# Two graph-attention layers on one Trainium2 core: holding the turning of each group's score row behind a partial sum on VectorE

## Chip, cores and metric

The kernel runs on one core of a Trainium2 chip. The metric is the device time of one launch in microseconds, taken as the median of several runs. All arithmetic is float32.

## What is computed

The input `x` is 64 graphs of 256 nodes with 512 features; `adj` is one 256 x 256 adjacency matrix for all of them. Two layers follow, each of the form `x = x + layer(relu(layernorm(x)), adj)`. Cut to what matters:

```python
# layer 0: additive attention
h = X @ W                                     # 512 -> 256
e = h @ a[0] + swap(h @ a[1])                 # one score per node pair
e = leaky_relu(e, 0.2) + NEG * (1 - adj)
alpha = softmax(e)
out0 = concat(alpha @ h, h)
# layer 1: multi-head attention, 8 heads of 64
q, k, v = X @ Wq.T + bq, X @ Wk.T + bk, X @ Wv.T + bv
attn = softmax(where(adj == 0, -inf, q @ k.T / 8))
out1 = (attn @ v) @ Wo.T + bo
```

## The kernel before

**Tiling.** The 64 graphs go through in 32 groups of two (`GB = 2`), numbered g = 0 to 31. The work of three groups is interleaved: while step (g, b) does layer 1's attention of graph b of group g, it also does the q, k, v projections of group g+1, layer 0 of group g+2 and the first norm of group g+3. The order inside a step is written out by hand: the strings `steps` (near the end of `bounded`) hold one letter for each piece of work, and the loop over them calls the next piece of the generator that the letter names ("s" is a piece of `first_layer(g + 2)`, "f" one of `fold`, "u" one of `project`, "o" one of `outputs`, "n" one of `first_norm`, "m" one of `mask_pairs`). Each group therefore has two half-steps, b = 0 and b = 1. A scheduler then decides the final order on each engine. Where the code calls `after(instruction, name)` or `not_sooner(...)`, an instruction is fixed behind another one on its engine without a semaphore.

**The row sums of the softmax (`fold`).** The masked exponentials `p` are summed over partitions in a detour. For each quad of four heads SyncE writes them to device memory (`rows<-p`), reads them back in another layout (`parts<-rows`, four transfers), GpSimd adds the parts in two additions (`add`), and VectorE turns the result and reduces it (`sum_up`: `parts<-parts`, a transpose of 128x256, then `compact<-parts`). The list `fold_last` then names that reduction. There are two quads, so two sums: only after `sum_up(0, ...)` does `fetch(1)` issue the second quad's four transfers. In the half b = 0 both quads' parts lie in the buffer with the tag `e`, of which there is one. The same buffer holds layer 0's score matrix (`both`, in the profile `e`).

**The score row of layer 0 (`first_products`, `score_rows`, `first_layer`).** For g >= 2, layer 0's product H = X W is made in seven block products; two VectorE additions write its last blocks (`H<-ph,kept_h`). Then `score_rows(g)` turns columns 0 to 7 of H on VectorE (`rows<-H`, a transpose of 128x32), SyncE writes the row to device memory (`line<-rows`), waits until it has landed, and reads it back to all partitions (`own<-line`). ScalarE then makes four pieces of `e` from it (`e<-own,H`), VectorE takes the leaky maximum (`e<-e`), ScalarE the exponential, and VectorE applies the mask (`e<-e,maskT`).

**Order around it.** On SyncE every transfer here is fixed in the program's order: `parts<-rows` of the second quad, then `line<-rows`, `own<-line`, `passed<-xt` (the first norm of group g+3), and `out_dram<-x`. In the program, `sum_up(0, ...)` of step g stands before `score_rows(g + 2)`; the scheduler places `rows<-H` and the statistics of the next norm (`st<-x`, `mv<-st`, `factor<-mv`) ahead of it on VectorE, except for group 2 (and, for group 3, ahead of its reduction only). On ScalarE the exponentials of the attention scores (`p<-sc`) are fixed behind `edge_last`, the exponential of `e`. The scores `sc` are made by TensorE in PSUM banks: five turn under the tag `turn`, and one of the eight score banks of a half-step is the separate `held2`.

`score_rows` is called in `first_products`, right after the addition that writes the last block of H:

```python
        product(second, 4, False)
        vector.tensor_add(part(1, 0), second, p16)
        owns[g] = score_rows(g)
        residual_from(1)
```

Of the kernel before, what the change touches and what calls it, by code (L numbers as in the profile page):

```python
# [57 lines left out]
def bounded(  # L58
# [56 lines left out]
    def after(instruction, name):  # L115

        tc.add_manual_dep(
            instruction.ins, name,
            mybir.DependencyInfo(mybir.DependencyClass.NoSync, mybir.DependencyReason.DATA),
            reason="the engine's order",  # L120
        )

    def not_sooner(engine, operation, *args, **kwargs):

        last = engine.last
        after(getattr(engine, operation)(*args, **kwargs), last)
# [143 lines left out]
    put_last, norm_last, edge_last, sums_last, turn_last, fold_last = [], [], [], [], [], []  # L270
# [350 lines left out]
    def score_rows(g):  # L621
        rows = small.tile([P, GT, 8], F32, tag="rows", name=f"rows_{g}", bufs=2)
        last = vector.last
        turned = vector.transpose(rows.rearrange("p t c -> p (t c)"), H[:, :, 0:8])
        for other in [last, *fold_last] if g == 2 else [last]:
            after(turned, other)
        line = dram.tile([P // 8, S], F32, tag="line", name=f"line_{g}")
        not_sooner(sync, "dma_start", line, rows.rearrange("p t c -> p (t c)")[::8, :])
        own = att.tile([P, P // S, GT, S], F32, tag="r", name=f"own_{g}", bufs=1)
        not_sooner(  # L630
            sync, "dma_start", own.rearrange("p k t j -> p (k t j)"),
            line.rearrange("(o k) j -> o (k j)", o=1).to_broadcast([P, TOK]),
        )
        return own.rearrange("p k t j -> p t k j")

    def first_products(g):
# [53 lines left out]
# [4 lines that stand above are left out]
        yield  # L694
# [908 lines left out]
```

## Time and profile before

| | |
|---|---|
| Median of 3 runs | 2425.27 us (2424.95 to 2428.83) |
| Profiled execution: its own time | 2427.43 us |
| Its span in the trace | 2425.8 us |
| TensorE busy | 2391.4 us (99%) |
| VectorE busy | 1712.9 us (71%) |
| GpSimd busy | 1431.3 us (59%) |
| ScalarE busy | 1020.1 us (42%) |
| `rows<-H` (VectorE transpose 128x32) | 30 times, 210 ns mean |
| `parts<-parts` (VectorE transpose 128x256) | 124 times, 439 ns mean |
| `compact<-parts` (VectorE reduction) | 124 times, 420 ns mean |
| `line<-rows`, `own<-line` (SyncE transfers) | 30 times each |

The page gives, for each engine, the time it was busy; then the chain of work that ended last, followed back from the last instruction; then the costliest groups of instructions, with the idle time of the engine before them and what ended it. A timeline line gives the start, the duration, the engine, the operation, what it writes and reads, and in brackets the idle time of the engine just before it. PE is TensorE, DVE is VectorE, ACT is ScalarE, POOL is GpSimd, SPq is the queue of SyncE.

### The profile page before, as it was taken

What the parts mean: (1) busy time and instruction counts of PE and PEld (TensorE: products, weight loads), DVE (VectorE), ACT (ScalarE), POOL (GpSimd) and SP (SyncE); (2) the same over time, 40 slices, a digit from 0 to 9 for tenths busy, and PEclk for the clock granted to TensorE, in tenths of its full rate; (3) what the DMA queues carried; (4) which work ended last, traced back from release to release, by engine and by line L of the source; (5) the groups of instructions that cost most, each with busy time, mean ns of one, the idle gap of its engine ahead of it and who ended that gap; (6) DMA issues with size and microseconds to landing.
All of it is one profiled execution on the core that took longest, in us unless ns stands there. A gap on an engine that the chain in (4) does not pass through costs nothing.

```text
span 2425.8 us, 43056 instructions
## 1 busy us (share of the span) xinstructions
PE 2391.4 (99%) x15828; PEld 2005.6 (83%) x15828; DVE 1712.9 (71%) x3345; ACT 1020.1 (42%) x2017; POOL 1431.3 (59%) x1290
## 2 busy tenths in 40 slices
PE   9999999999999999999999999999999999999998
PEld 8888888888888888888888888888888888888886
DVE  7577776676766777667767677776677676777665
ACT  5444444343443443444444434444344344343431
POOL 4565555755656655566555565565665566655652
PEclk9999999999999999999999999999999999999999
DMA  5344445454445544455444545444554445454331
GB/s 187 126 139 144 144 133 154 145 159 140 132 139 149 169 143 134 130 161 148 144 144 134 154 144 160 147 130 134 152 166 144 135 135 158 143 156 138 112 114 45
DMA packets 271864, 343.49 MB, mean 142 GB/s; under 512 B 25376, under 2 KB 217120, under 8 KB 271648
## 3 DMA queue, kind: packets, MB, share of 16 engines
q1 hardware_dynamic: 271648, 340.69, 46.0%
q8 instruction: 126, 2.06, 0.4%
q14 instruction: 90, 0.74, 0.1%
HBM read 176.95 MB, written 163.64 MB: 140 GB/s over the span
## 4 chain that ended last, share of the span: by engine, by line
PE 87%; DMA 4%; DVE 3%; ACT 3%; issue 2%; POOL 1%; SPq 0%; ACTq 0%; DVEq 0%; POOLq 0%
PE pq L137 16%; PE pv L137 16%; PE py L137 14%; PE pk L137 14%; PE sc L137 8%; PE ph L137 8%; PE pr L137 6%; PE po L137 4%; ACT e L35 2%; DMA passed<-xt 1%; DMA own<-line 1%; DVE e L35 1%; DVE p L35 1%; ACT p L35 1%; DMA line<-rows 0%
## 5 line engine op out<-in xcount | busy, mean ns | idle before, releaser
L35 POOL TENSOR_TENSOR p<-p 128x512 f32<-128x512 f32 x248 | 392.9, 1598 | 453.6 <-DVE p L35 451.0
L35 ACT ACTIVATE xn<-x,factor 128x512 f32<-128x512 f32 x256 | 194.7, 807 | 384.4 <-POOL factor L35 377.3
L35 DVE TENSOR_TENSOR p<-p,maskT 128x1024 f32<-128x1024 f32 x254 | 347.5, 1389 | 3.2 <-ACT p L35 3.2
L35 POOL TENSOR_TENSOR parts<-parts 128x512 f32<-128x512 f32 x248 | 248.0, 1000 | 158.8 <-DMA parts<-rows 147.4
L35 DVE TENSOR_TENSOR x<-py,x 128x256 f32<-128x256 f32 x448 | 184.4, 412 | 179.8 <-PE py L137 173.6
L35 ACT ACTIVATE p<-sc 128x512 f32<-128x512 f32 x512 | 256.9, 620 | 88.5 <-PE sc L137 72.1
L137 PE MATMUL sc<-q,k 64*128 64x256 f32 x2048 | 255.1, 386 | 22.0 <-ACT p L35 22.0
L137 PEld LDWEIGHTS sc<-q,k 64*128 64x128 f32 x2048 | 201.3, 186 | 76.4 <-ACT p L35 34.2
L137 PE MATMUL py<-wo_sb,oT 128*128 128x256 f32 x1024 | 262.4, 379 | 0.6 <-DVE oT L35 0.6
L137 PE MATMUL pk<-hT,wk_sb 128*128 128x256 f32 x1024 | 244.8, 382 | 0.0
L137 PE MATMUL pq<-hT,wq_sb 128*128 128x256 f32 x1024 | 240.1, 382 | 1.1 <-ACT hT L35 0.7
L137 PE MATMUL pv<-wv_sb,hT 128*128 128x256 f32 x1024 | 236.8, 379 | 0.0
L137 PE MATMUL pr<-p,v 128*32 128x256 f32 x4096 | 234.2, 380 | 0.0
L137 PEld LDWEIGHTS pq<-hT,wq_sb 128*128 128x128 f32 x1024 | 191.8, 190 | 36.7 <-issue 10.3
L137 PEld LDWEIGHTS py<-wo_sb,oT 128*128 128x128 f32 x1024 | 194.2, 190 | 28.2 <-DVE oT L35 1.1
L137 PEld LDWEIGHTS pk<-hT,wk_sb 128*128 128x128 f32 x1024 | 189.7, 190 | 33.3 <-issue 9.9
L137 PEld LDWEIGHTS pv<-wv_sb,hT 128*128 128x128 f32 x1024 | 194.6, 190 | 26.5
L137 PEld LDWEIGHTS pr<-p,v 128*32 128x32 f32 x4096 | 126.7, 110 | 97.8 <-issue 18.2
L35 POOL TENSOR_TENSOR factor<-factor,rexp 128x2 f32<-128x2 f32 (+1 forms) x132 | 117.9, 893 | 150.2 <-DVE factor L35 149.8
L137 PE MATMUL py<-wo_sb,o_sums 128*128 128x256 f32 x768 | 197.6, 380 | 0.5 <-DVE x L35 0.5
L137 PE MATMUL pv<-wv_sb,sums 128*128 128x256 f32 x768 | 184.3, 383 | 2.2 <-ACT kept_v L35 2.2
L137 PE MATMUL pq<-sums,wq_sb 128*128 128x256 f32 x768 | 181.5, 379 | 0.0
(150 smaller groups left out, 4075.8 us busy)
## 6 DMA issues: line engine op xcount, KB each, us to landing
passed<-xt SPq DMA_DIRECT2D x124, 512.0 KB, 3.8
moved<-passed SPq DMA_DIRECT2D x496, 128.0 KB, 3.4
rows<-p SPq DMA_DIRECT2D x124, 512.0 KB, 3.4
parts<-rows SPq DMA_DIRECT2D x496, 128.0 KB, 3.0
x<-in_x_dram SPq DMA_DIRECT2D x64, 512.0 KB, 4.4
out_dram<-x SPq DMA_DIRECT2D x62, 512.0 KB, 4.4
own<-line SPq DMA_DIRECT2D x30, 256.0 KB, 3.5
wq_sb<-in_L_gnn_Wq_dram SPq DMA_DIRECT2D x2, 512.0 KB, 9.1
```

Source lines behind the costliest of these rows:

```text
L35: instruction = getattr(self.engine, operation)(*args, **kwargs)
L137: in_order(nc.tensor.matmul(*args, **kwargs))
```

## The change

`score_rows` already holds the turning of the row behind the last reduction of `fold` (`fold_last`) for group 2. The change does this for every group from 2 on.

```diff
         turned = vector.transpose(rows.rearrange("p t c -> p (t c)"), H[:, :, 0:8])
-        for other in [last, *fold_last] if g == 2 else [last]:
+        for other in [last, *fold_last] if g >= 2 else [last]:
             after(turned, other)
```

When `score_rows` is called, `fold_last` names the reduction of the first quad of the half b = 0. No instruction is added or removed. In the built program the order on TensorE, ScalarE, GpSimd and SyncE is the same as before; on VectorE it differs in 29 places, one for each of the groups 3 to 31. For groups 4 to 30 it goes from

```
rows<-H, st<-x, mv<-st, st<-x, mv<-st, factor<-mv x2, parts<-parts, compact<-parts, x<-py, k<-pk
```

to

```
parts<-parts, compact<-parts, rows<-H, st<-x, x<-py, mv<-st, st<-x, mv<-st, factor<-mv x2, k<-pk
```

For group 3 only `compact<-parts` moves, from behind the first `st<-x` to just ahead of `rows<-H`. For group 31, which has no norm beside it, `rows<-H` moves from just ahead of `parts<-parts` to just behind `compact<-parts`.

## The prediction

> **What bounds the kernel now.** I began with the page. TensorE is busy for 99% of the span, and the group of score products is the one large group on it with idle time of its own.
>
> ```profile
> PE 2391.4 (99%) x15828; PEld 2005.6 (83%) x15828; DVE 1712.9 (71%) x3345; ACT 1020.1 (42%) x2017; POOL 1431.3 (59%) x1290
> ...
> L137 PE MATMUL sc<-q,k 64*128 64x256 f32 x2048 | 255.1, 386 | 22.0 <-ACT p L35 22.0
> ```
>
> The reader sees that only what makes TensorE wait can move the time, and that a wait of the scores for ScalarE's exponentials is such a thing. Next I read the chain of waits in order of time over one group (step g = 15, where the score row of group 17 is made).
>
> ```profile
> 1201.61 3.65 PE sc L137 x32
> 1205.26 7.10 PE pq L137 x32
> ...
> 1234.37 3.40 DMA passed<-xt
> ...
> 1237.86 1.72 ACT e L35 x4
> ...
> 1240.87 0.59 ACT p L35
> ...
> 1241.50 2.26 PE sc L137 x15
> ```
>
> In the half b = 0 the 32 score products run through in 3.65 us. In the half b = 1 the chain leaves TensorE, goes over a transfer, `e` and the first exponential, and comes back to the 17th score product. In TensorE's timeline the scores of b = 1 start at 1238.57 and the matmul behind them at 1243.69: 5.12 us, so 1.47 us are lost. (The page's 22.0 us counts less, since the ends of matmuls are modelled; I use distances between starts.) I read this distance in every half-step. In b = 0 it is always 3.65 from group 2 on; in b = 1 it is 4.59 to 5.81 for g = 2 to 28, so 0.94 to 2.16 lost, mean 1.34, in all 36.2 us; for g = 0 and 1 the loss is 0.71 and 0.70, and for g = 29 it is 0.09.
>
> Then VectorE and SyncE's queue before that wait.
>
> ```profile
> 1225.99 0.21 DVE L35 STREAM_TRANSPOSE rows<-H 128x32 f32<-128x32 f32 x1
> 1226.13 0.65 DVE L35 BATCH_NORM_STATS2 st<-x 128x6 f32<-128x512 f32 x1
> ...
> 1227.83 0.62 DVE L35 TENSOR_SCALAR factor<-mv 128x2 f32<-128x2 f32 x2
> 1228.36 0.43 DVE L35 STREAM_TRANSPOSE parts<-parts 128x256 f32<-128x256 f32 x1
> 1228.82 0.42 DVE L35 TENSOR_REDUCE compact<-parts 128x8 f32<-128x256 f32 x1
> 1229.16 0.42 DVE L35 TENSOR_TENSOR x<-py,x 128x256 f32<-128x256 f32 x1
> ```
>
> ```profile
> 1229.32 1.73 SPq L35 DMA_DIRECT2D parts<-rows  x4
> 1231.09 0.53 SPq L35 DMA_DIRECT2D line<-rows  x1
> 1233.98 0.34 SPq L35 DMA_DIRECT2D own<-line  x1
> 1234.37 0.43 SPq L35 DMA_DIRECT2D passed<-xt  x1
> ```
>
> The row is turned at 1226.2, but its transfer stands in SyncE's queue behind the second quad's four fetches, and those wait for the first quad's reduction, which ends at 1229.24. So turning the row early gains nothing: 0.08 us after the reduction the queue moves, and `line` is issued 4.9 us after the row was ready. `e` starts at 1237.86. The chain names `passed<-xt`, but `e` does not read it; `own` takes 3.0 to 3.9 us to land (its tile's view), so its landing, 1237.0 to 1237.9, is what I take as the end of that wait.
>
> **What the skill says.** The Trainium skill, "Perfetto Trace Analysis", § Optimization Strategy, says to look for gaps on the limiting engine and trace who releases them, and that a gap that keeps repeating can mean a lack of SBUF or PSUM. Agreed: here it repeats in 27 groups and the 17th score product waits for a score bank to be read. "DMA: Bandwidth & Descriptors", § Anatomy of one DMA, says that a wait on a semaphore is done by the issuing sequencer ahead of dispatch. Agreed: `own` leaves 2.89 us after `line` and `passed` right behind it, so one waiting transfer holds all behind it.
>
> **The change part by part.** Nothing is added or removed; all of it is order on VectorE.
>
> *Sum ahead of the row.* The parts must be there. GpSimd's two additions start at 1221.22 and take 2.07, so they end at 1223.29, 2.67 us before the addition to H ends (1225.96). In all of g = 4 to 28 this lead is 2.4 to 2.7 us, so the new wait costs nothing; without that lead, `rows` and all behind it on VectorE would wait with it, 1 us for 1 us. The transpose then starts at 1225.99, the reduction at 1226.45, and it ends at 1226.87 instead of 1229.24: 2.37 us sooner. The row is turned at 1226.79 to 1227.0, 0.8 us later, but `line` cannot go before the fetches anyway.
>
> *SyncE.* Fetches at 1226.95, `line` at 1228.72, `own` 2.89 behind it at 1231.61; `own` to `e` took 3.88 (1233.98 to 1237.86), so the row allows `e` at 1235.49. `passed` waits for `xt` instead and leaves near 1234, not later than now.
>
> *The other gate of `e`.* `e` shares its buffer with the second quad's parts. Fetch to GpSimd took 4.58 (1229.32 to 1233.90): 1231.53; plus 2.08 is 1233.61. VectorE's order puts the sum behind an `x<-py` that waits for TensorE and starts at 1235.08. With the spacings of the trace (0.34, 0.47, 0.42) the reduction ends at 1236.31, and `e` starts 0.09 later at 1236.40. That is what is late next: 1.46 us sooner than now, not 2.37, and the same place relative to TensorE in every group.
>
> *What is pushed back.* The statistics follow 0.86 us later (0.46 for the transpose and its spacing, 0.34 for the reduction, rounding), and `x<-py` now stands in their midst: its four matmuls end at 1229.00, so VectorE waits there to about 1229.05. Two aggregations, one `st` (0.65) and two `factor` follow, to about 1230.7 instead of 1228.45. GpSimd took `factor` only at 1229.54 (behind `x` and `v`), so it loses 1.2 us: 1231.6 for both operations, `xn` on ScalarE (1.52) 1231.75 to 1233.3. ScalarE's next work is `kept_k` at 1234.28, so 1.0 us of cover is left; the second `xt` moves to 1234.0, ahead of the `x<-py` of 1235.08. GpSimd is free at 1231.6 for parts that land at 1231.53: hidden by the 1.5 us to 1235.08. Cost taken: nothing; its bounds are 0 and, with no cover, 1.2 us a group, which would eat most of the gain. Below nothing it can't go, as no statistic comes sooner.
>
> *What a group gains.* The last group before the end of this pattern shows it, since it has no statistics between row and sum:
>
> ```profile
> 2269.21 0.21 DVE L35 STREAM_TRANSPOSE rows<-H 128x32 f32<-128x32 f32 x1
> 2269.42 0.45 DVE L35 STREAM_TRANSPOSE parts<-parts 128x256 f32<-128x256 f32 x1
> 2269.90 0.42 DVE L35 TENSOR_REDUCE compact<-parts 128x8 f32<-128x256 f32 x1
> ...
> 2278.30 0.42 DVE L35 TENSOR_TENSOR x<-py,x 128x256 f32<-128x256 f32 x1 [2.17 <-PE py L137]
> ...
> 2279.11 0.42 DVE L35 TENSOR_REDUCE compact<-parts 128x8 f32<-128x256 f32 x1
> ```
>
> ```profile
> 2281.79 3.81 PE L137 MATMUL sc<-q,k 64*128 64x256 f32 x32
> ```
>
> There the second reduction ends at 2279.53, `e` starts at 2279.62, 2.17 us ahead of the scores, as 1236.40 is ahead of 1238.57. The scores pass without a wait, 3.74 us to the next matmul: 0.09 lost instead of 1.34. So 27 groups x (1.34 - 0.09) = 33.8 us. For group 3 only the reduction moves, by some 0.5 us; its step loses 0.70 now, so I take 0.5, from 0 to 0.6. Group 31: `rows` 0.9 us later, hidden behind the fetches: 0. Group 2 is as it was. Sum: 34.3 us. Behind the scores VectorE and ScalarE follow `e`, and TensorE's later work comes sooner by as much as they do, so nothing should take it back.
>
> Against the profiled execution's own time: 2427.43 - 34.3 = 2393.1. It lies 2.2 above the median of the runs; the difference belongs to the runs, so 2425.27 - 34.3 = **2391.0**.
>
> **The rivals.** (a) *Part of it*: the row, not the second sum, still ends last in many groups. For it: `line` to `e` varies (an `own` that lands late, fetches that issue slowly: in g = 1 four of them took 2.92 instead of 1.73, and its reduction, already early at -11.3 us from the scores, did not let `e` start before -1.47). Against: 0.9 us lies between 1235.49 and 1236.40. If a third of the gain stays lost: 2425.3 - 23 = 2402. (b) *No effect*: the gap only moves to the next thing, as `x<-py` or `po`. For it: VectorE runs without a break from 1238.8 to beyond 1258. Against: that stretch starts with `e`, and g = 29 shows no such gap. 2425. (c) *Slower*: the `x<-py` in the midst of the statistics holds `factor`, `xn` gets behind `kept_k` on ScalarE, and `e` behind both. It begins to cost when `xn` ends 1.0 us later than I put it, and outweighs the gain when it holds `e` back beyond 1237.86; there are 1.28 us between the end of `kept_k` (1235.12) and 1236.40, and 1.46 of gain, so from 3.7 us on. With 4.2 us: 27 x 0.5 = 13.5, so 2439. Against: the `x<-py` waits for TensorE at a known place.
>
> **How the numbers follow.** The forecast has a chance of 0.74 (2387 to 2397: the 36.9 us that are there at most, and 28 of them), (a) 0.17, (b) 0.04, (c) 0.05. About 0.2% (5 us) is what a measurement of this kernel can tell from no change. Faster by more: 0.74 + 0.17 = 0.91; within: 0.04; slower: 0.05. The range reaches from 2387 to 2404, over most of (a).
>
> **What would show it.** Right: `compact<-parts` ends about 0.9 us after the addition to H, `parts<-rows` is issued 11.6 us ahead of the scores of b = 1 instead of 9.2, `e<-own` starts 2.2 us ahead of them instead of 0.0 to 1.2, and their distance to the next matmul is 3.7 to 3.8 us. Wrong: `e` still released by `own`, `kept_k` late behind `xn`, or new idle time of TensorE at `po`, `pk` or `pr`.

## The result and the profile after

| | before | after |
|---|---|---|
| Median of 5 runs | 2425.27 us (2424.25 to 2429.59) | 2390.06 us (2389.08 to 2391.81) |
| Span of the profiled execution | 2425.8 us | 2388.3 us |
| Distance from the first score product of b = 1 to the matmul behind the scores, g = 2 to 28 | 4.59 to 5.81 us | 3.74 us in every step |

The ratio is 0.9851 (95% interval 0.9836 to 0.9865): 35.2 us less. The same lines as before, first the page:

```profile
PE 2375.2 (99%) x15828; PEld 1993.8 (83%) x15828; DVE 1705.2 (71%) x3345; ACT 1023.0 (43%) x2017; POOL 1430.5 (60%) x1290
...
L137 PE MATMUL sc<-q,k 64*128 64x256 f32 x2048 | 241.9, 385 | 0.1
```

The score products' own idle time has gone from 22.0 to 0.1 us. The chain of waits in order of time, for the same group of work as before (step g = 15, which now lies 19 us earlier):

```profile
1182.90 3.65 PE sc L137 x32
1186.56 7.10 PE pq L137 x32
...
1219.93 3.74 PE sc L137 x32
1223.67 1.92 PE pk L137 x8
```

The detour over a transfer, `e` and an exponential is no longer in it: the scores of b = 1 run through. VectorE's timeline shows the new order, and SyncE's the queue behind it:

```profile
1206.83 0.43 DVE L35 TENSOR_TENSOR H<-ph,kept_h 128x258 f32<-128x258 f32 x1 [0.40 <-PE ph L137]
1207.17 0.44 DVE L35 STREAM_TRANSPOSE parts<-parts 128x256 f32<-128x256 f32 x1
1207.64 0.42 DVE L35 TENSOR_REDUCE compact<-parts 128x8 f32<-128x256 f32 x1
1207.98 0.20 DVE L35 STREAM_TRANSPOSE rows<-H 128x32 f32<-128x32 f32 x1
1208.10 0.65 DVE L35 BATCH_NORM_STATS2 st<-x 128x6 f32<-128x512 f32 x1
1210.33 0.42 DVE L35 TENSOR_TENSOR x<-py,x 128x256 f32<-128x256 f32 x1 [1.58 <-PE py L137]
...
1211.68 0.24 DVE L35 TENSOR_SCALAR factor<-mv 128x2 f32<-128x2 f32 x2
...
1216.38 0.42 DVE L35 TENSOR_TENSOR x<-py,x 128x256 f32<-128x256 f32 x1 [0.86 <-PE py L137]
...
1217.19 0.42 DVE L35 TENSOR_REDUCE compact<-parts 128x8 f32<-128x256 f32 x1
```

```profile
1208.13 1.73 SPq L35 DMA_DIRECT2D parts<-rows  x4
1209.90 0.53 SPq L35 DMA_DIRECT2D line<-rows  x1
1212.86 0.34 SPq L35 DMA_DIRECT2D own<-line  x1
1215.23 0.34 SPq L35 DMA_DIRECT2D passed<-xt  x1
```

The first sum follows the addition to H at once, the fetches leave 0.07 us after it, and the row leaves behind them. ScalarE's timeline shows the two things that could have spoiled it:

```profile
1212.94 1.52 ACT L35 ACTIVATE xn<-x,factor 128x512 f32<-128x512 f32 x2 [2.57 <-POOL factor L35]
1215.57 0.84 ACT L35 ACTIVATE kept_k<-pk,bk_sb 128x256 f32<-128x256 f32 x2 [1.11 <-PE pk L137]
1217.69 1.71 ACT L35 ACTIVATE e<-own,H 128x256 f32<-128x256 f32 x4 [1.28 <-DMA passed<-xt]
```

The norm `xn` is later than before, but still 1.1 us ahead of `kept_k`, and `e` starts at 1217.69, right after the second reduction (1217.19 + 0.42 = 1217.61). The name in brackets is again not the cause: `passed` is not read by `e`.

Where the time went, from the starts of TensorE's matmuls in both traces: the losses inside the scores of b = 1 fall from 36.2 to 2.4 us over g = 2 to 28 (33.8), and from 1.4 to 0.7 for g = 0 and 1 (0.7). The stretch from the scores of b = 1 to those of the next half-step, freed of that loss, is 2.3 us shorter in all, by 0.07 to 0.11 us in each step from 1 to 28 but g = 4. Together that is 36.8 of the 37.5 us between the spans. Another 0.6 lies in the first half of step g = 1, ahead of the first row that the change moves, so it belongs to the execution and not to the change. The spans differ by more than the medians because the profiled execution of before (2427.43 us) lies 2.2 us above its median.

### The profile page after: what moved, and what is told of

Same layout as the page of the kernel before. It is cut to its first block, busy times and chain, and to the rows that moved or that the text cites. A ratio compares the mean times of both kernels' runs of the same rounds, so it can differ in the third digit from the quotient of the medians.

```text
span 2388.3 us, 43029 instructions
## 1 busy us (share of the span) xinstructions
PE 2375.2 (99%) x15828; PEld 1993.8 (83%) x15828; DVE 1705.2 (71%) x3345; ACT 1023.0 (43%) x2017; POOL 1430.5 (60%) x1290
## 4 chain that ended last, share of the span: by engine, by line
PE 95%; DVE 2%; ACT 1%; issue 1%; DMA 0%; POOL 0%; SPq 0%; DVEq 0%; ACTq 0%; POOLq 0%
PE pq L137 16%; PE pv L137 16%; PE py L137 16%; PE pk L137 15%; PE sc L137 10%; PE pr L137 9%; PE ph L137 8%; PE po L137 4%; DVE p L35 1%; DMA a_b<-in_L_gnn_a_dram 0%; ACT xn L35 0%; DVE x L35 0%; DVE st L35 0%; ACT e L35 0%; PE total L137 0%
## 5 line engine op out<-in xcount | busy, mean ns | idle before, releaser
L137 PE MATMUL sc<-q,k 64*128 64x256 f32 x2048 | 241.9, 385 | 0.1
L137 PEld LDWEIGHTS sc<-q,k 64*128 64x128 f32 x2048 | 190.8, 187 | 51.8 <-issue 26.3
L137 PEld LDWEIGHTS pq<-hT,wq_sb 128*128 128x128 f32 x1024 | 191.8, 190 | 36.7 <-issue 10.3
```

The costliest lines, as they stand in the source:

```text
L137: in_order(nc.tensor.matmul(*args, **kwargs))
```

## The experiments

All times below in "us from the scores" count from the first score product of b = 1 (a minus is ahead of it) and are means over g = 2 to 28 unless said otherwise. What a step loses is the distance from that product to the matmul behind the scores, less 3.65 us. Each ratio is to the kernel before on the same chip. The theory: `e` waits for the row, which stands in SyncE's queue behind the second quad's fetches, and those wait for the first sum; 0.6 us ahead of the row (means -1.60 and -1.04) comes the second sum, which frees `e`'s buffer. The rivals: only the row's way matters (1), or SyncE's order is beside the point and the sum's place on VectorE counts in itself (2).

**The row ahead of the fetches, in the kernel before.** VectorE's order stays that of before from group 4 on; the fetch is made a piece of its own behind the row (the other strings alike).

```diff
         sum_up(0, parts)
+        yield
         parts = fetch(1)
...
-    steps = ("Smmnfuuuumonmnuofuusssosfsfssuvnofunonfosuo", ...
+    steps = ("Smmnfuuuumonmnuofuusssosfsfsfsuvnofunonfosuo", ...
```

> VectorE's order of before is kept (the row is turned early, the sum comes after the statistics); only on SyncE the row's two transfers now stand ahead of the second quad's fetches. Theory (the score matrix e waits for two things: first the row, which stood behind the fetches, and 0.3 to 0.9 us ahead of it the second sum, which frees its buffer): the row lands some 6 us ahead of the scores, so the second sum ends last. Its fetches now leave after own, at about -9.0 us from the scores of b = 1, the reduction ends at -1.4, e starts at -1.3, and 0.9 us a step are lost instead of 1.34: 2413 us (2405 to 2420). Rival 1 (only the row's way matters): e starts at -2.2 or sooner, 2390. Rival 2 (SyncE's order is beside the point, the place of the sum on VectorE is what counts): 2425.

Measured: 2425.96 us, ratio 1.0002 (0.9995 to 1.0009). The time is that of rival 2, the trace is not: the row lands at -6.9, `e` starts 0.08 us after the second reduction, at -1.09 instead of -0.83. In VectorE's timeline of step g = 15 the second sum waits for GpSimd, which adds what the fetches bring:

```profile
1241.78 0.42 DVE L35 TENSOR_TENSOR x<-py,x 128x256 f32<-128x256 f32 x1 [1.51 <-PE py L137]
1242.93 0.45 DVE L35 STREAM_TRANSPOSE parts<-parts 128x256 f32<-128x256 f32 x1 [0.73 <-POOL parts L35]
1243.41 0.42 DVE L35 TENSOR_REDUCE compact<-parts 128x8 f32<-128x256 f32 x1
```

The trace is of the slowest of the 20 executions (2430.49 us). In it a step loses 1.14 us instead of 1.34 (the median step 0.87, as expected), so 27 steps gain 5.4; but g = 0 and 1 lose 11.1 us instead of 1.4, since there the fetches leave 2.9 and 3.4 us later. I had left those two steps out of the estimate. And the fetches now stand behind `own`, which waits until `line` has landed and so leaves anywhere from 1.8 to 3.8 us after it. The mechanism is as said, the size of 2413 was wrong. In most of the 27 steps the fetches leave no later than before (median -9.25 in both kernels), but they land later, at -4.37 instead of -4.79; the next experiment shows more of this.

**The same edit in the changed kernel.**

> The changed kernel with the same edit on SyncE: the row's transfers ahead of the second quad's fetches. Theory: line leaves at -11.6 us from the scores of b = 1, own 2.9 later, so the fetches leave at -8.3 instead of -11.7, the second reduction ends at -0.7 and e starts at -0.6: 1.6 us a step lost, 2431 us, slower than before. Rival 1 (only the row's way matters): the row lands even sooner, 2390. Rival 2 (only the place of the sum on VectorE counts): 2390.

Measured: 2448.52 us, ratio 1.009 (1.0073 to 1.0107): the sum is as early on VectorE as in the change and the row lands sooner (-6.2 instead of -3.8), and yet the kernel is slower than before. The second reduction ends at -0.57, `e` starts at -0.49, a step loses 1.78 us, g = 0 and 1 lose 10.3 together. Both rivals said 2390, so both fall: the sum's place helps only through the fetches that it lets go.

That the reduction ends near the -0.7 that I expected is luck. The fetches left at -9.27 and not at -8.3, which is no later than in the kernel before (-9.25); but they landed at -3.76, where before they landed at -4.79. So what makes this run slower than the kernel before, in these steps, is not when the fetches leave but how long they take, 0.58 us behind the read of the row to all partitions. Why they take longer there was not tried.

**A buffer of its own for `e`, in the kernel before.** `e` no longer shares a buffer with the parts of the sums; it takes its turn in the two buffers of the tag `moved`. Every order stays as before.

```diff
-        both = att.tile([P, GB, NT, N], F32, tag="e", name=f"e_{g}", bufs=1)
+        both = att.tile([P, GB, NT, N], F32, tag="moved", name=f"e_{g}")
```

> The kernel before, in which e no longer shares its buffer with the parts of the sums (it takes its turn in the two buffers of moved). Every order is as before. Theory: e waited for the row there, so nothing changes: 2425 us, e starts at 0.0 to -1.2 us from the scores. Rival (the second sum ended last already): e starts up to 0.9 us sooner, 2405 to 2415.

Measured: 2420.09 us, ratio 0.9978 (0.9969 to 0.9988): neither. The view of the tile `e` now names the row alone as the transfer that ended a wait of ScalarE:

```profile
  DMA own<-line: 66.2, 28
```

So the row did end last. But `e` now starts 0.02 us after it has landed, where before it started 0.21 after it (-0.83 and -1.04); a step loses 1.11 instead of 1.34, 6.1 us in all. Before, the first instruction of `e` waits for nine semaphores (signals of other engines and transfers), and here for one. The records of ScalarE in the trace of before show what that costs: ahead of `e` stand four instructions that only wait, for two semaphores each, and after the row has landed those that stand behind the row's own place in the list still run one after another, 0.077 us apart. Here there is none of them. So most of the 0.23 us that `e` gains is this list, and not the second sum itself, which ends at -1.60 before and -1.61 here.

**Both at once, in the kernel before.**

> The kernel before with both: the row's transfers ahead of the fetches, and e in a buffer of its own. The sum stays late on VectorE, as before. Theory: both of e's waits are gone without the change, e starts when ScalarE is free, 3.4 us ahead of the scores, and the step loses some 0.1 us: 2390 us, as the change. Rival 2 (the place of the sum on VectorE counts in itself): 2425.

Measured: 2385.44 us, ratio 0.9833 (0.9817 to 0.985). The first sum ends at -9.3 as before, `e` starts at -6.5 in front of the `kept_k` copies, and a step loses 0.09. It is 4.6 us faster than expected; the last experiment shows where such a gain lies. With both of its waits gone, the gap closes without the change; the sum's time on VectorE has no part of its own in it.

**The row not held, the statistics held.** The kernel before, with the first statistic of each next norm from group 4 on held behind the sum.

```diff
-            not_sooner(vector, "bn_stats", st, src[t])
+            others = [vector.last]
+            if name[:2] == "0_" and t == 0 and int(name[2:]) > 3:
+                others += fold_last
+            made = vector.bn_stats(st, src[t])
+            for other in others:
+                after(made, other)
```

> The row is turned early, as before, but the first statistics of the next norm are held behind the sum: on VectorE rows, parts, compact, st, where the changed kernel has parts, compact, rows, st. Nothing else differs from the changed kernel. Theory: it is the time of the sum that counts, not that the row waits for it; the reduction ends 0.1 us later than in the changed kernel and 1.4 us are to spare: 2390 us. Rival (the row itself has to be held): 2425.

Measured: 2389.66 us, ratio 0.9867 (0.985 to 0.9883), on another chip, where the kernel before takes 2421.93 us. VectorE's timeline:

```profile
1206.59 0.21 DVE L35 STREAM_TRANSPOSE rows<-H 128x32 f32<-128x32 f32 x1
1206.79 0.45 DVE L35 STREAM_TRANSPOSE parts<-parts 128x256 f32<-128x256 f32 x1
1207.27 0.42 DVE L35 TENSOR_REDUCE compact<-parts 128x8 f32<-128x256 f32 x1
```

The reduction ends at -11.47, 0.33 us later than in the change (said: 0.1). `e` starts at -2.17, as in the change, with the row turned 0.7 us sooner. What the change does is to bring the sum ahead of the statistics; that the row waits is only how.

**Spare transfers, first try.** In the changed kernel, 2 and then 5 transfers of a constant on SyncE between the first sum and the fetches.

> The changed kernel with 2 spare transfers of 2 KB on SyncE between the first sum and the second quad's fetches, in b = 0; no other engine's order differs. They hold the fetches and the row back by about 1.06 us. Theory: e waits for the sum that stands behind an addition fed by TensorE; the row has 1.5 us to spare and the second quad's parts 1.7, so nothing changes: 2390 us (2389 to 2393). Rival (e follows the fetches or the row one to one): 27 x 1.06 = 29 us more, 2419.

> The same with 5 spare transfers, about 2.65 us. Theory: that is 1.2 us more than the row has to spare, its landing moves to -1.15 us from the scores, e starts at -0.9, 1.3 us a step are lost as before the change, though VectorE's order is that of the change: 2423 us (2412 to 2430). Rival 2 (the place of the sum on VectorE counts in itself): 2390.

Measured: 2389.64 and 2389.38 us (0.9867 and 0.9865). These tell nothing on the theory: nothing held the transfers to the sum, so they left while the queue was idle, 8 us ahead of the fetches, and those left at -11.73 as in the change. So they were made again to read the sum:

```diff
         sum_up(0, parts)
+        if b == 0:
+            for i in range(5):
+                spare = dram.tile([P // 8, N // S], F32, tag="spare", name=f"spare_{g}_{i}")
+                not_sooner(sync, "dma_start", spare, compact[::8, 0])
         parts = fetch(1)
```

> The changed kernel with 2 spare transfers that read the first sum, so that they can't leave before it, between it and the second quad's fetches in b = 0 (in the runs before, spare transfers of a constant left while the queue was idle and held nothing back). They hold the fetches and the row back by about 1.06 us (0.53 each, as line takes). Theory: the row has 1.5 us to spare and the second quad's parts 1.7, so nothing changes: 2390 us (2389 to 2393). Rival (e follows the fetches or the row one to one): 29 us more, 2419.

Measured: 2400.51 us, ratio 0.9894 (0.9878 to 0.9911). The two held the queue for 1.39 us, not 1.06, and `own` took 3.5 us to land, not 3.2: the fetches leave at -10.34, the row lands at -2.10, 1.70 us later than in the change, and `e` starts at -1.97. That is just past the slack; 4.2 us more are lost in 27 steps than in the change, 3.4 in g = 0 and 1, the rest mostly behind the scores. My slack of 1.5 us left out the 0.1 to 0.3 us that pass here between the landing and `e`.

> The same with 5 such transfers, about 2.65 us. Theory: the row's landing moves from -3.8 to -1.15 us from the scores, e starts at -0.9, 1.3 us a step are lost as before the change though VectorE's order is that of the change: 2423 us (2412 to 2430). Rival 2 (the place of the sum on VectorE counts in itself): 2390.

Measured: 2473.26 us, ratio 1.0202 (1.0183 to 1.0221): more than expected. SyncE's and TensorE's timelines in step g = 15:

```profile
1248.99 3.06 SPq L35 DMA_DIRECT2D spare<-compact  x5
1252.21 1.88 SPq L35 DMA_DIRECT2D parts<-rows  x4
1254.19 0.48 SPq L35 DMA_DIRECT2D line<-rows  x1
1256.98 0.34 SPq L35 DMA_DIRECT2D own<-line  x1
```

```profile
1260.77 2.00 PE L137 MATMUL sc<-q,k 64*128 64x256 f32 x16
1264.22 2.26 PE L137 MATMUL sc<-q,k 64*128 64x256 f32 x16 [1.45 <-ACT p L35]
```

The five hold the queue 3.2 us, not 2.65, and `own` takes 3.6 us to land, not 3.2, so the row lands at -0.06 instead of -1.15; `e` starts at +0.17 and a step loses 2.65 us. VectorE's order around the sum is that of the change, the kernel is slower than before: the delay was put on SyncE alone, and the same gap came back, larger.

**Every other group.** The kernel before with `if g % 2 == 0`.

> The change for the even groups alone: 14 of the 27 steps whose gap it closes. Theory (each step's gap is its own, nothing is given back later): 14/27 of the gain, 18 us: 2425 - 18 = 2407 (2404 to 2410), and in the trace the loss alternates between 0.09 and 0.9 to 2.2 us. Rival (a step that ends sooner runs into the next one's wait): clearly less than half of the gain.

Measured: 2407.19 us, ratio 0.9921 (0.9905 to 0.9938). Two score stretches of b = 1, one without and one with the change, in the chain of waits:

```profile
1230.67 1.94 PE sc L137 x16
...
1232.62 0.59 ACT p L35
...
1233.25 2.26 PE sc L137 x15
...
1305.04 3.74 PE sc L137 x32
```

In the 13 steps left as they were the loss stays at 0.9 to 2.1 us, in the others it is 0.09: 14 of 27 gaps closed give half of the gain, and no step takes back what another gained.

**A buffer of its own for `e`, with the change, and with the statistics held.**

> The changed kernel with e in a buffer of its own: the second sum no longer holds e. Theory: e starts up to 1.2 us sooner, when the row lands, but the exponentials of the scores then wait for the scores themselves, and the 0.09 us that a step still loses stays: 2390 us (2388 to 2391). Rival (the second sum still costs): down to 2387.

> The row turned early, the statistics held behind the sum, and e in a buffer of its own. e can start at -3.6 us from the scores, as in the changed kernel with a buffer of its own (2384). Theory: nothing is left to gain at the scores, the copy of the values' first product no longer comes late either, so it gives the same: 2384 us (2382 to 2386).

Measured: 2384.03 us, ratio 0.9843 (0.9826 to 0.9859), and 2385.03 us, ratio 0.9834 (0.9818 to 0.9851). The first ran on the same chip as the one with the statistics held, which took 5.6 us more (2389.66), so it beats the change's order; my "2388 to 2391" was wrong. The second ran on a third chip; its interval overlaps that of the change, but its trace shows the same gain at the same place. The scores lose 0.09 us as they did; the gain is at TensorE's products of the values 17 us later, here in step g = 15, first before the change, then with it, then with the buffer:

```profile
1260.21 1.03 PE L137 MATMUL py<-wo_sb,oT 128*128 128x256 f32 x4
1261.18 1.99 PE L137 MATMUL pv<-wv_sb,sums 128*128 128x256 f32 x8
1263.01 1.03 PE L137 MATMUL py<-wo_sb,o_sums 128*128 128x256 f32 x4
```

```profile
1240.13 1.03 PE L137 MATMUL py<-wo_sb,oT 128*128 128x256 f32 x4
1241.01 1.99 PE L137 MATMUL pv<-wv_sb,sums 128*128 128x256 f32 x8
1242.84 1.03 PE L137 MATMUL py<-wo_sb,o_sums 128*128 128x256 f32 x4
```

```profile
1236.61 1.03 PE L137 MATMUL py<-wo_sb,oT 128*128 128x256 f32 x4
1237.48 1.89 PE L137 MATMUL pv<-wv_sb,sums 128*128 128x256 f32 x8
1239.20 1.03 PE L137 MATMUL py<-wo_sb,o_sums 128*128 128x256 f32 x4
```

From the first start to the third it is 2.80, 2.71 and 2.59 us. Added up over the run, the distances between these three starts give 5.4 of the 5.8 us by which the spans of the change and of the first buffer run differ: 0.12 to 0.13 in nearly every step and 0.65, 0.66 and 1.07 in steps 2, 3 and 6. ScalarE's timeline shows the other side, first with the change, then with the buffer:

```profile
1238.97 1.52 ACT L35 ACTIVATE xn<-x,factor 128x512 f32<-128x512 f32 x2 [1.03 <-POOL factor L35]
1240.40 0.56 ACT L35 COPY kept_v<-pv 128x512 f32<-128x512 f32 x1
```

```profile
1234.37 1.52 ACT L35 ACTIVATE xn<-x,factor 128x512 f32<-128x512 f32 x2 [1.03 <-POOL factor L35]
1235.80 0.56 ACT L35 COPY kept_v<-pv 128x512 f32<-128x512 f32 x1
```

With the change the copy starts 0.27 us after the first of the three products, with the buffer 0.81 us before it. There `pv` waits for ScalarE's copy `kept_v`, which stands behind `xn`, which waits for `factor`, which comes at the end of VectorE's unbroken stretch of work that `e` opens. What `e` gains beyond the scores' need arrives there. That each link passes it on is read from the timelines; no run tests the links one by one.

## Why the prediction was right

- *The sum is ready and costs no wait.* GpSimd's parts end at -15.3 to -14.8 us from the scores, the addition to H at -12.61. Right in all 27 steps.
- *The reduction comes 2.37 us sooner.* It ends at -11.80 instead of -9.32: 2.48, since the transpose, which does not read H, starts 0.09 us before the recorded end of the addition, where I had it 0.03 us behind. The fetches leave at -11.73 (said: 11.6 ahead).
- *The row then allows `e` at 1235.49*, which is -3.1. It lands at -3.80; `own` took 3.2 us (median of its tile's view) instead of 3.5, with `passed` leaving 2.4 us behind it and not 0.4. On the safe side, and not the gate.
- *The second sum is late next, at the same place in every group.* `e` starts at -2.17 in each of the 27 steps, 0.08 us after the reduction that stands behind the `x<-py` fed by TensorE.
- *The statistics are pushed back and it costs nothing.* They follow 0.68 us later, not 0.86 (whose named parts add up to 0.80). VectorE's `factor` ends at -7.94 (said: -7.9), `xn` at -5.40 (said: -5.3), `kept_k` keeps its time at -4.29. The wait of `x<-py` is there, 1.58 us, ending at 1210.33.
- *27 x 1.25 = 33.8 us*: measured 33.8. *Group 3, 0.5*: measured 0.61.
- *"Nothing should take it back"*: nothing did, but 2.3 us came on top, 0.08 a step. The step that fell short is the sentence that TensorE's later work comes sooner by as much as VectorE and ScalarE do. TensorE came sooner by the loss at the scores; in the traces the copy `kept_v`, measured from the products next to it, comes another 0.08 us sooner, and TensorE had been waiting for it. For the same reason "the 36.9 us that are there at most" was no bound: it counts the losses at the scores alone, and the run with the buffer gained 37.9 us on its chip. (2425.27 less 36.9 is 2388.4, not 2387.)
- *The total.* The terms as predicted add up to 34.3 and measured 34.4; with the 2.3 us at the values it is 36.7. The medians differ by 35.2; that this lies so near the forecast is in part luck, as executions of before alone range over 5 us.
- *The rivals.* (a) the row last: not in one step, though little is to spare: from its landing to `e` it is 1.63 us in the mean and 0.57 in the tightest step, and with the two spare transfers, which moved the row by 1.70, it ends last. (b) the gap moves: no. (c) `xn` behind `kept_k`: 1.1 us were left, as said (1.0).

## What to carry to other kernels

An instruction that produces data early gains nothing while the transfer that carries it stands in a queue behind one that waits; look for what the head of the queue waits for, and bring that forward. When two things end a wait, cost both: freeing only the later one gives the distance to the other, and here freeing it by reordering the queue made the other one later. A group at the end or the start of the loop that lacks part of the pattern can be a measurement of the changed state that the old profile already holds, as g = 29 was here.

## What was not expected of the hardware

- A list of waits cost time even where one of them ended long after the others. Before, `e` began 0.10, 0.18, 0.34 and 0.22 us after its row had landed, in this order over and over from step to step, and 0.02 us when it waited for one semaphore (`own_buffer_before`). In the records the row always comes last, but its place in the list turns with the step: one, two, four or three of the waiting instructions were still to run after the landing, each 0.038 us long and 0.077 us from the next. In the run with five spare transfers the order is another one, and there too the delay grows with that count, from 0.10 to 0.34 us (one step excepted).
- Small transfers on SyncE (16 rows of 32 bytes) took 0.6 us of its queue each (five in 3.06 us), no less than one of 2 KB (0.53).
- Two transfers on SyncE that left close together took longer. The score row, 2 KB read to all partitions, landed in 3.2 us with nothing close behind it and in 3.5 us with a 512 KB transfer issued 0.4 us later (medians); in `every_other`, within one execution, 3.23 and 3.54 us (means of 14 and 13 steps). The other way round, the second quad's fetches (four of 128 KB) took 2.6 to 3.2 us each before, and 3.8 to 4.2 us where they left 0.58 us behind that read (`row_first_after`). What the two share was not tried.
